# Contiguous operands in an edge sort, carried sums added once in DRAM, and a bias added by VectorE instead of TensorE

## The chip, the cores and the metric

The kernel runs on one core of one Trainium2 chip. Its time is the device time of one execution in microseconds (us), given as the median of several runs. The core has five engines with a queue of instructions each: TensorE (PE in the profile; PEld is its loading of weights), VectorE (DVE), ScalarE (ACT), GpSimd (POOL) and SyncE (SP). In this kernel SP issues the plain DMAs and POOL issues the indirect ones, which gather or scatter one row for each of 128 partitions.

## The reference

The reference is a graph block over 3125 nodes with 256 features. A normalised input goes through a message passing network over 103125 edges that are sorted by their target, and through a transformer of four layers with linear attention. Both are added to the input. On the sum, an attention over 65536 unsorted edges chooses two of four experts for each node, and each expert is a two-layer network.

```python
xn = _layernorm(x)
# message network: edges sorted by receiver (dst)
messages = concat(xn[src], edge_attr) @ W_message
agg = segment_sum(messages, dst, 3125)
h = layer_norm(relu(agg) + xn); three linear layers with skips; layer_norm
# transformer: 4 layers of linear attention (softmax of k over all nodes) + gelu feed-forward 256 -> 1024 -> 256
x = x + gnn + mix
# graph attention over 65536 unsorted edges gives scores for 4 experts
e = leaky_relu(a_src[src] + a_dst[dst]); alpha = segment softmax of e over dst
scores = layernorm(segment_sum(h[src] * alpha)); top 2 of 4, softmax
for ei in range(4):
    hh = gelu(xf @ W1[ei] + b1[ei])                 # 256 -> 512
    out = out + g[..., None] * (hh @ W2[ei] + b2[ei])   # 512 -> 256
x = x + out
```

## The kernel before

**Tiles.** The 3125 nodes are 25 tiles of 128 (the last holds 53), and they are worked on in seven chunks of up to four tiles (`CHUNKS`). The message edges lie on 128 partitions with 806 columns each; a partition holds a contiguous run of sorted edges. The attention's edges lie on 128 partitions with 512 columns each, which are worked on in 64 groups of eight columns (`GC`).

**The main line.** TensorE follows the transformer's four layers, chunk by chunk, with `ff_up` (L1101, then a gelu on ACT at L1102) and `ff_down` (L1112, added up at L1115). All other work is let in between by a planner: `pace()` adds up the planned time of what has been issued and lets in message columns (`run_columns`), pieces of message nodes and sends, and `beside()` takes jobs from a list. The order within each engine's queue follows from this, with some reordering when the program is compiled.

**The message sums.** POOL gathers a row of `xn` for each of the 806 columns (L478), and DVE adds each to a running sum that starts anew at a new target (L490). The running sums are written to `run_d` in DRAM. A node's sum is the running sum at its last edge. Since a target's edges can begin in one partition and end in the next, the last running sums of all partitions (`last_m`) are carried over. The nodes are then worked on in pairs of tiles (`pair`, a generator that is advanced piece by piece at each `yield`): `fetch` gathers the sums from `run_d` at the rows `sum_i` (L559), a mask `goes_on` (L569) times `last_m` gives the carried part (L571), L572 masks the fetched row by `has_m` and adds that part, and L575 adds `part`, which is read from `res_d`. Row block 0 of `res_d` is zero; the other blocks are filled only if the edges came unsorted, and `flag` picks which is read. After this follow transposes (L585), the message product (L593), three linear layers (L609 to L612), a normalisation, and the next `fetch`, three pairs ahead.

**The edge sort.** The attention's edges are brought in the order of their targets by counting. The target's number is split in `hi` (128 values) and `lo` (32 values). `count_group` makes one-hots of both by `one_hot` (L668, laid out as value by column, so that one column is read at a step of eight elements), multiplies them column by column (L683), has ACT copy the counts (L685), writes them to `counts_d` and adds them to `table` (L690). `place_group` reads the counts back (`parts`), turns them into running counts by a scan on DVE (L728), and adds up in one PSUM tile `look` for each edge how many come earlier: L746 with a constant, and at L753 eight products each with `near`, `run` and `earlier`. DVE picks each edge's own value at L755 and L756, and `laid` turns it into a place (`place`). ACT makes `earlier` from products at L740 by a Sign (L741). `send` (L770) scatters each column of edges to its place in `by_dst`, 512 times.

**The end of the mix.** `finish` adds the message network's result to `xm` (L805), normalises, and makes the attention's table (`tab`, L818 and L819).

**The experts.** `expert(e)` takes the chunks in turn: L1301 and a gelu (L1303), then for two tiles at a time L1309, which puts the second bias into PSUM as a product of ones with three bf16 parts of the bias (`bias_rows`, L145 to L151), and L1312. ACT takes the result out of PSUM (L1315 and L1317). Between them stand 16 edge chunks (`gathered`, L1211; `edge_chunk`, L1232 to L1269, with two exponentials on ACT at L1223). A tile with a `tag` shares the buffer of that tag with an earlier tile and must wait for its readers:

```python
be2s = [bias_rows(so, a["L0_ffn_b2"][e], f"be2{e}", tags) for e, tags in enumerate((
    ("own_bin", "lo", "base"), ("own_bin", "hi", "base"), ("own_bin", "place", "base"), ("own_bin", "ohT0", "base")))]
```

The functions that the diff touches, with the profile's line numbers:

Of the kernel before, what the change touches and what calls it, by code (L numbers as in the profile page):

```python
# [8 lines left out]
F32 = mybir.dt.float32  # L9
BF16 = mybir.dt.bfloat16  # L10
I32 = mybir.dt.int32
# [7 lines left out]
P = 128  # L19
# [39 lines left out]
def kernel(ctx: ExitStack, tc: tile.TileContext, a: dict, out: bass.AP):  # L59
# [124 lines left out]
    mi = mi_open.enter_context(tc.tile_pool(name="mi", bufs=1))  # L184
    res_d = dram.tile([P + NP, DM], F32, name="res_d")
    run_d = dram.tile([EP, DM], F32, name="run_d")
# [140 lines left out]
    nc.sync.dma_start(res_d[:P, :].rearrange("p (a b) -> p a b", b=160), zero[:, :160].rearrange("p (o c) -> p o c", o=1).to_broadcast([P, 2, 160]))  # L327
    pairs0 = so.tile([P, TE], I32, name="pairs0", tag="pairs")
# [25 lines left out]
    G.iota(bin_p, pattern=[[0, 1]], base=0, channel_multiplier=1, allow_small_or_imprecise_dtypes=True)  # L354
    ident_h = const.tile([P, P], F16, name="ident_h")
# [23 lines left out]
    has_m = state.tile([P, NT], F32, name="has_m")  # L379
# [7 lines left out]
    sums_ps = px.tile([P, LO * GC + 2 * NT], F32, name="sums_ps")  # L387

    table, whole_ps, first_ps = sums_ps[:, :LO * GC], sums_ps[:, LO * GC:LO * GC + NT], sums_ps[:, LO * GC + NT:]
# [33 lines left out]
    def ends_sum():  # L423
# [11 lines left out]
        cnt_d = dram.tile([1 + NP, 1], F32, name="cnt_d")  # L435
# [4 lines left out]
    def ends_done():  # L440
        V.tensor_tensor(has_m, cnt, own_n, op=ALU.is_gt)
        V.tensor_scalar(has_m, has_m, in_order, None, op0=ALU.mult)
        V.tensor_scalar(cnt, cnt, -1.0, 0.0, op0=ALU.add, op1=ALU.max)
        V.tensor_scalar(sum_i, cnt, float(EP - 1), None, op0=ALU.min)
# [56 lines left out]
    last_gather = [None]  # L501
# [38 lines left out]
    def message_nodes():  # L540
# [23 lines left out]
        def pair(c):  # L564
            agg = fetched[c[0]]
            k, n0, w = len(c), c[0] * P, len(c) * P
            for i, t in enumerate(c):
                goes_on = wk2.tile([P, P], F32, name="goes_on")
                V.tensor_scalar(goes_on, ids, last_t[:, t:t + 1], cont, op0=ALU.is_equal, op1=ALU.mult)  # L569
                ps = pg.tile([P, DM], F32, name="ps_g")  # L570
                T.matmul(ps, goes_on, last_m, start=True, stop=True)  # L571
                V.scalar_tensor_tensor(agg[:, i, :], agg[:, i, :], has_m[:, t:t + 1], ps, op0=ALU.mult, op1=ALU.add)  # L572
                part = wk2.tile([P, DM], F32, name="part", bufs=2)
                nc.sync.dma_start(part, res_d[bass.ds(flag * (P * (t + 1)), P), :])
                V.tensor_tensor(agg[:, i, :], agg[:, i, :], part, op=ALU.add)  # L575
                yield False
# [62 lines left out]

        for c in PAIRS[:3]:  # L640
            fetch(c)
# [29 lines left out]

    counts_d = dram.tile([GROUPS, P, LO * (GC + 1)], F16, name="counts_d")
# [5 lines left out]
    def count_group(t):  # L678
        if t < TE:
            ohh, ohl = one_hot(t, hi, P, "oh_hi", 2), one_hot(t, lo, LO, "oh_lo", 3)  # L680
            ps = pg.tile([P, LO, GC], F32, name="ps_g")
            for i in range(GC):
                T.matmul(ps[:, :, i], ohh[:, :, i], ohl[:, :, i], start=i == 0, stop=i == GC - 1, skip_group_check=True)  # L683
            cnt = cnts[t // GC % 2]
            S.copy(cnt[:, :, 1:], ps)  # L685
            nc.sync.dma_start(counts_d[t // GC, :, :], cnt.rearrange("p l i -> p (l i)"))
            counted.append((t, cnt))
        if t:
            t, cnt = counted.pop(0)
            T.matmul(table, ident_h, cnt[:, :, 1:], start=t == 0, stop=t + GC == TE, skip_group_check=True)  # L690
# [6 lines left out]
    def parts(t):  # L697
        cnt = so.tile([P, LO, GC + 1], F16, name="run", bufs=3)
# [3 lines left out]
    def starts():  # L702
        cnt2 = so.tile([P, LO], F32, name="cnt2", tag="base")
        V.tensor_reduce(cnt2, table.rearrange("p (l i) -> p l i", i=GC), AX.X, ALU.add)
# [13 lines left out]
    def place_group(t):  # L718

        late = looks.pop() if looks else None  # L720
        if t < TE:
# [4 lines left out]
            ohl = one_hot(t, lo, LO, "oh_lo", 3)  # L726
            near, run = places.pop()
            V.tensor_tensor_scan(run.rearrange("p l i -> p (l i)"), goes.rearrange("p l i -> p (l i)"),  # L728
                                 run.rearrange("p l i -> p (l i)"), 0.0, op0=ALU.mult, op1=ALU.add)
            if t + GC < TE:  # L730
                base = so.tile([P, LO], F32, name="base")
                V.tensor_tensor(base, run[:, :, GC], near, op=ALU.add)
# [10 lines left out]
        if late:  # L743
            t, ohT, ohl, near, run, earlier = late
            look = pg.tile([P, GC, LO], F32, name="ps_g")
            T.matmul(look.rearrange("p i l -> p l i"), all_h, ohl, start=True, stop=False, skip_group_check=True)  # L746
            for k in range(3):
                for i in range(GC):
                    if k == 2:
                        a1, a2 = earlier[:, i, :], ohl[:, :, i]  # L750
                    else:
                        a1, a2 = ohT[:P - 1, i, :], run[:P - 1, :, i] if k else near[:P - 1]
                    T.matmul(look[:, i, :], a1, a2, start=False, stop=k == 2, skip_group_check=True)  # L753
            own = so.tile([P, GC, LO], F32, name="own_bin", bufs=1)
            V.scalar_tensor_tensor(own, look, float(E2), ohl.rearrange("p l i -> p i l"), op0=ALU.add, op1=ALU.mult)  # L755
# [140 lines left out]
    def zero_fills():  # L896
        nothing = so.tile([P, TE], I32, name="nothing", tag="hr", bufs=2)
# [198 lines left out]
    def ff_up(l, c, h2, f0, f1):  # L1096
        w = len(c) * P
# [192 lines left out]
    def expert(e):  # L1290
# [4 lines left out]
        for c in CHUNKS:  # L1295
# [9 lines left out]
            for i0 in range(0, len(c), 2):  # L1305
# [3 lines left out]
                T.matmul(ps[:, :k, :], ones_b, be2[:, :k, :], start=True, stop=False, skip_group_check=True)  # L1309
                for i in range(k):  # L1310
                    for f in range(FF2 // P):
                        T.matmul(ps[:, i, :], hh[f][:, (i0 + i) * P:(i0 + i + 1) * P], we2[:, f, :],  # L1312
                                 start=False, stop=f == FF2 // P - 1, skip_group_check=True)
# [247 lines left out]
```

## Time and profile before

| what | value |
|---|---|
| median of 3 runs | 3781.26 us (3776.46 to 3784.04) |
| own time of the profiled execution | 3726.91 us |
| its span | 3725.2 us |
| mean granted TensorE clock | 0.762 |
| message gathers, L478 | 806 of 989 ns |
| sends, L770 | 512 of 966 ns |
| edge gathers, L1211 | 400 of 952 ns |

The profiled execution is some 54 us (1.4%) faster than the median of the runs shown. Its stages, in microseconds from the start of the span: start and normalisation 0 to 192, layer 0 to 930, layer 1 to 1472, layer 2 to 2333 (with an overlap of stages at its start), layer 3 and `finish` to 2892, experts and edge chunks to 3610, gates and output to 3725. The message gathers run from 42 to 1637, the count groups from 198 to 434, the place groups from 641 to 2766, the message nodes' pairs from 1687 to 2672 and the sends from 1638 to 2810.

A line of the profile gives the place of the instruction in the kernel (L12), its engine and operation, the tiles written and read, and the shapes. In a group's line follow the number of instructions, then busy time in us and the mean in ns of one, then the idle time of the engine just before them and what ended it. "issue" is time in which an engine waited for nothing that the profile shows, and "remote" is a release that the profile ascribes to no instruction. In a line of the timeline the first number is the start in us from the start of the span, the second the duration of the row, and the bracket at the end the idle time before it.

### The profile page before, as it was taken

How to read it: one execution, taken by the hardware profiler on the slowest of the kernel's cores; microseconds unless marked ns; L12 is line 12 of the kernel's file. 1: busy time of each engine (PE TensorE's matmuls, PEld its weight loads, DVE VectorE, ACT ScalarE, POOL GpSimd, SP SyncE). 2: the span in 40 equal slices, each digit the busy share in tenths (PEclk: the TensorE clock that was granted, in tenths of full speed). 3: DMA queues.
4: the chain of work that ended last, by engine and by line, in shares of the span. 5: the costliest groups of instructions: out<-in, count | busy, mean ns of one | idle time of the engine just before them, and what ended most of it. 6: DMA issues, size and time to landing. Idle time of an engine off the chain costs nothing. (4 is left out here: it accounts for less than half of the span.)

```text
span 3725.2 us, 31745 instructions
## 1 busy us (share of the span) xinstructions
PE 2232.7 (60%) x9891; PEld 1505.7 (40%) x9891; DVE 1452.2 (39%) x4484; ACT 1062.2 (29%) x1933; POOL 1776.0 (48%) x1843
## 2 busy tenths in 40 slices
PE   3667654675667676645575466547667275747470
PEld 2545433443444455433343344435445143424250
DVE  6656544644544455532232233324422021111127
ACT  4422242233233233322232224213333021212122
POOL 2545454544445544644435434453442736464623
PEclk8878776776778887877787777768788677868685
DMA  6656564746645556722010002101100101010101
GB/s 206 193 188 201 162 199 136 211 157 192 212 150 190 176 166 209 225 80 77 20 33 18 23 18 58 43 25 35 44 10 8 16 17 30 15 29 14 27 12 36
DMA packets 300669, 359.57 MB, mean 97 GB/s; under 512 B 180576, under 2 KB 248039, under 8 KB 287687
## 3 DMA queue, kind: packets, MB, share of 16 engines
q1 hardware_dynamic: 229782, 242.00, 20.4%
q0 software_dynamic: 70704, 115.42, 11.9%
q8 instruction: 80, 1.31, 0.1%
q14 instruction: 103, 0.84, 0.1%
HBM read 201.91 MB, written 155.35 MB: 96 GB/s over the span
## 5 line engine op out<-in xcount | busy, mean ns | idle before, releaser
L478 POOL DMA_INDIRECT m_run<-xn_d,src_i x806 | 797.5, 989 | 835.9 <-issue 228.2
L770 POOL DMA_INDIRECT by_dst<-pairs,place x512 | 494.8, 966 | 280.3 <-issue 185.5
L1211 POOL DMA_INDIRECT rows_c<-tab_d,si x400 | 380.6, 952 | 301.5 <-DVE rows_c L1269 182.6
L1101 PE MATMUL ps_a<-h,w 128*128 128x512 f32 (+1 forms) x896 | 413.0, 604 | 101.5 <-ACT gT L1102 38.5
L490 DVE SCALAR_TENSOR_TENSOR m_run<-m_run,stay 128x320 f32<-128x320 f32 x805 | 437.3, 543 | 32.3 <-DMA m_run<-xn_d,src_i 17.7
L1112 PE MATMUL ps_a<-w,gT 128*128 128x256 f32 x1600 | 382.3, 394 | 20.4 <-issue 19.9
L1112 PEld LDWEIGHTS ps_a<-w,gT 128*128 128x128 f32 x1600 | 314.4, 198 | 124.2 <-issue 78.4
L1301 PE MATMUL ps_a<-hT,we 128*128 128x512 f32 (+1 forms) x448 | 226.5, 640 | 137.9 <-issue 115.1
L1101 PEld LDWEIGHTS ps_a<-h,w 128*128 128x128 f32 x896 | 173.8, 214 | 267.5 <-issue 189.5
L1312 PE MATMUL ps_t<-we,hf 128*128 128x256 f32 x800 | 203.7, 406 | 111.6 <-issue 79.1
L609 PE MATMUL ps_a<-gh,gw 128*128 128x256 f32 (+1 forms) x312 | 106.4, 489 | 207.7 <-DVE gh L612 95.8
L1312 PEld LDWEIGHTS ps_t<-we,hf 128*128 128x128 f32 x800 | 160.2, 204 | 158.5 <-issue 97.9
L1301 PEld LDWEIGHTS ps_a<-hT,we 128*128 128x128 f32 x448 | 89.7, 213 | 294.0 <-issue 259.2
L1102 ACT ACTIVATE gT<-ps_a,b 128x512 f32<-128x512 f32 (+1 forms) x224 | 141.3, 641 | 214.3 <-PE ps_a L1101 118.8
L1261 DVE COPY rows_c<-ev 128x104 f32<-128x104 f32 (+1 forms) x16 | 4.6, 286 | 481.7 <-ACT ev L1223 471.3
L559 POOL DMA_INDIRECT aggr<-run_d,sum_i x25 | 24.4, 977 | 336.2 <-PE ps_t L585 312.9
L609 PEld LDWEIGHTS ps_a<-gh,gw 128*128 128x128 f32 x312 | 72.7, 250 | 235.9 <-DVE gh L612 102.2
L741 ACT ACTIVATE earlier<-ps_t,slope 128x512 f16<-128x512 f32 x128 | 93.8, 773 | 260.0 <-PE ps_t L740 146.2
L1039 PE MATMUL ps_g<-xm,kr 128*128 128x256 f32 x400 | 127.5, 463 | 63.8 <-ACT kr L1037 36.1
L123 ACT ACTIVATE hn<-xm,rstd 128x256 f32<-128x256 f32 x225 | 121.4, 592 | 86.5 <-DVE rstd L119 57.7
L1039 PEld LDWEIGHTS ps_g<-xm,kr 128*128 128x128 f32 x400 | 88.4, 232 | 118.3 <-ACT kr L1037 58.5
L159 PE MATMUL ps_t<-ident,hn 128*128 128x128 f32 x450 | 82.7, 319 | 87.6 <-issue 37.7
(399 smaller groups left out, 3615.6 us busy)
## 6 DMA issues: line engine op xcount, KB each, us to landing
run_d<-m_run SPq DMA_DIRECT2D x100, 1280.0 KB
m_run<-in_edge_attr_dram SPq DMA_DIRECT2D x95, 256.0 KB
hr<-row_h SPq DMA_DIRECT2D x64, 256.0 KB
m_run<-xn_d,src_i POOLq DMA_INDIRECT x806
w<-in_L_mix_W_dram SPq DMA_DIRECT2D x8, 1024.0 KB
by_dst<-pairs,place POOLq DMA_INDIRECT x512
rows_c<-tab_d,si POOLq DMA_INDIRECT x400
run_d<-rows_c SPq DMA_DIRECT2D x15, 312.0 KB
```

The lines of the kernel that those rows point to most:

```text
L123: S.activation(dst, src, AF.Identity, bias=r[:, 1, i:i + 1], scale=r[:, 0, i:i + 1])
L478: last_gather[0] = G.indirect_dma_start(out=m[:, t, :D], out_offset=None, in_=xn_d, in_offset=bass.IndirectOffsetOnAxis(ap=src_i[:, t0 + t ...
L490: add = V.scalar_tensor_tensor(m[:, t, :], before_m, stay[:, c:c + 1], m[:, t, :], op0=ALU.mult, op1=ALU.add)
L609: T.matmul(ps[:, :w], gw[i][:, kc, m * P:(m + 1) * P], h[:, kc, :w], start=kc == 0, stop=kc == 1)
L770: i = G.indirect_dma_start(out=by_dst, out_offset=bass.IndirectOffsetOnAxis(ap=place[:, t:t + 1], axis=0), in_=pairs0[:, t:t + 1], in_offs ...
L1039: T.matmul(ps_x[:, m, :], kr[:, m * P:(m + 1) * P], xm[:, t, :], start=i == 0 and m == 0, stop=i == len(c) - 1, skip_group_check=True)
L1101: T.matmul(ps[:, :w], ff_w[l]["w1"][:, kc, f * P:(f + 1) * P], h2[:, kc, :w], start=kc == 0, stop=kc == 1)
L1102: S.activation(gT[:, f, :w], ps[:, :w], AF.Gelu, bias=ff_w[l]["b1"][:, f:f + 1])
L1112: T.matmul(ps[:, i, :], gT[:, f, (2 * i0 + i) * P:(2 * i0 + i + 1) * P], ff_w[l]["w2"][:, f, :], start=False, stop=f == FF // P - 1, skip_ ...
L1211: G.indirect_dma_start(out=rows_c[:, t - COLS[j], :], out_offset=None, in_=tab_d, in_offset=bass.IndirectOffsetOnAxis(ap=si[:, t:t + 1], a ...
L1301: T.matmul(ps[:, :w], we1[:, kc, f * P:(f + 1) * P], hT[:, kc, c[0] * P:c[0] * P + w], start=kc == 0, stop=kc == 1)
L1312: T.matmul(ps[:, i, :], hh[f][:, (i0 + i) * P:(i0 + i + 1) * P], we2[:, f, :], start=False, stop=f == FF2 // P - 1, skip_group_check=True)
```

## The change

It has four parts.

1. In the sort, `low_hots` lays the one-hots of `lo` out as column by value, so that one column is contiguous; the counts' PSUM tile and the products L683, L746 and L753 follow. ACT's copy of the counts writes at a step of nine elements in place of DVE's and PE's strided reads, `table` has nine columns a value instead of eight, and in `place_group` ACT copies the scanned `run_l` to a contiguous `run_c`.
2. The carried sums are added once in DRAM: `carries` multiplies `last_m` by a mask `joined`, and one indirect DMA adds the result to the rows `carry_i` of `run_d`, before the first fetch. `ends_done` works out `carry_i`, and gives nodes without edges the zero row `NO_SUM`. The blocks that were read as `part` are copied behind `run_d` by 25 DMAs from DRAM to DRAM (in `zero_fills`). `pair` loses its first loop with a `yield` for each tile. With unsorted edges `sum_i` points to the copied rows.
3. The experts' second bias is a tile of 128 equal rows, loaded by SP; DVE adds it as it takes results out of PSUM. The bias products and `be2s` by `bias_rows` go.
4. `ff_up` leaves out the columns beyond node 3125 in the last chunk.

```diff
-    run_d = dram.tile([EP, DM], F32, name="run_d")
+    run_d = dram.tile([EP + NP + 1 + P, DM], F32, name="run_d")
...
     def ends_done():
-        V.tensor_tensor(has_m, cnt, own_n, op=ALU.is_gt)
-        V.tensor_scalar(has_m, has_m, in_order, None, op0=ALU.mult)
-        V.tensor_scalar(cnt, cnt, -1.0, 0.0, op0=ALU.add, op1=ALU.max)
-        V.tensor_scalar(sum_i, cnt, float(EP - 1), None, op0=ALU.min)
+        V.tensor_tensor(own_n, cnt, own_n, op=ALU.is_gt)
+        V.tensor_scalar(cnt, cnt, float(-1 - NO_SUM), None, op0=ALU.add)
...
+        V.tensor_tensor(sum_i, cnt, node_n, op=ALU.add)
+        at_i = small.tile([P, 1], I32, name="at_i", bufs=1)
+        V.tensor_scalar(at_i, lastd, 1.0, float(NP), op0=ALU.add, op1=ALU.min)
+        at = small.tile([P, 3], F32, name="at_end_of", bufs=1)
+        last_gather[0] = G.indirect_dma_start(out=at[:, 0:1], out_offset=None, in_=ends_at["d"],
+                                              in_offset=bass.IndirectOffsetOnAxis(ap=at_i, axis=0))
...
+        T.transpose(ps[:, :P], joined, ident)
...
+        T.matmul(ps[:, :1], sooner, ones[:, :1], start=True, stop=True)
...
+    def carries(pool):
+        ps = pg.tile([P, DM], F32, name="ps_g")
+        T.matmul(ps, joined, last_m, start=True, stop=True)
+        over = pool.tile([P, DM], F32, name="over")
+        V.tensor_copy(over, ps)
+        last_gather[0] = G.indirect_dma_start(out=run_d, out_offset=bass.IndirectOffsetOnAxis(ap=carry_i[:, :1], axis=0),
+                                              in_=over, in_offset=None, compute_op=ALU.add)
...
         def pair(c):
             agg = fetched[c[0]]
             k, n0, w = len(c), c[0] * P, len(c) * P
-            for i, t in enumerate(c):
-                goes_on = wk2.tile([P, P], F32, name="goes_on")
-                V.tensor_scalar(goes_on, ids, last_t[:, t:t + 1], cont, op0=ALU.is_equal, op1=ALU.mult)
-                ps = pg.tile([P, DM], F32, name="ps_g")
-                T.matmul(ps, goes_on, last_m, start=True, stop=True)
-                V.scalar_tensor_tensor(agg[:, i, :], agg[:, i, :], has_m[:, t:t + 1], ps, op0=ALU.mult, op1=ALU.add)
-                part = wk2.tile([P, DM], F32, name="part", bufs=2)
-                nc.sync.dma_start(part, res_d[bass.ds(flag * (P * (t + 1)), P), :])
-                V.tensor_tensor(agg[:, i, :], agg[:, i, :], part, op=ALU.add)
-                yield False
...
+        carries(wk2)
         for c in PAIRS[:3]:
             fetch(c)
...
+    def low_hots(t):
+        o = so.tile([P, GC, LO], F16, name="oh_lo", bufs=3)
+        V.tensor_tensor(o, low_ids.rearrange("p (o l) -> p o l", o=1).to_broadcast([P, GC, LO]),
+                        lo[:, t:t + GC].rearrange("p (t o) -> p t o", o=1).to_broadcast([P, GC, LO]), op=ALU.is_equal)
+        return o
...
     def count_group(t):
         if t < TE:
-            ohh, ohl = one_hot(t, hi, P, "oh_hi", 2), one_hot(t, lo, LO, "oh_lo", 3)
-            ps = pg.tile([P, LO, GC], F32, name="ps_g")
+            ohh, ohl = one_hot(t, hi, P, "oh_hi", 2), low_hots(t)
+            ps = pg.tile([P, GC, LO], F32, name="ps_g")
             for i in range(GC):
-                T.matmul(ps[:, :, i], ohh[:, :, i], ohl[:, :, i], start=i == 0, stop=i == GC - 1, skip_group_check=True)
+                T.matmul(ps[:, i, :], ohh[:, :, i], ohl[:, i, :], start=i == 0, stop=i == GC - 1, skip_group_check=True)
             cnt = cnts[t // GC % 2]
-            S.copy(cnt[:, :, 1:], ps)
+            S.copy(cnt[:, :, 1:].rearrange("p l i -> p i l"), ps)
...
-            T.matmul(table, ident_h, cnt[:, :, 1:], start=t == 0, stop=t + GC == TE, skip_group_check=True)
+            T.matmul(table, ident_h, cnt.rearrange("p l i -> p (l i)"), start=t == 0, stop=t + GC == TE, skip_group_check=True)
...
+            run = so.tile([P, GC, LO], F16, name="run_c", tag=f"counts{t // GC % 2}")
+            S.copy(run, run_l[:, :, :GC].rearrange("p l i -> p i l"))
...
-            T.matmul(look.rearrange("p i l -> p l i"), all_h, ohl, start=True, stop=False, skip_group_check=True)
+            T.matmul(look, all_h, ohl, start=True, stop=False, skip_group_check=True)
...
-                        a1, a2 = earlier[:, i, :], ohl[:, :, i]
+                        a1, a2 = earlier[:, i, :], ohl[:, i, :]
                     else:
-                        a1, a2 = ohT[:P - 1, i, :], run[:P - 1, :, i] if k else near[:P - 1]
+                        a1, a2 = ohT[:P - 1, i, :], run[:P - 1, i, :] if k else near[:P - 1]
...
     def zero_fills():
+        nc.sync.dma_start(run_d[DUMP:DUMP + P, :].rearrange("p (a b) -> p a b", b=160),
+                          zero[:, :160].rearrange("p (o c) -> p o c", o=1).to_broadcast([P, 2, 160]))
+        for t in range(NT):
+            nc.sync.dma_start(run_d[FALLEN + t * P:FALLEN + (t + 1) * P, :], res_d[bass.ds(flag * (P * (t + 1)), P), :])
...
     def ff_up(l, c, h2, f0, f1):
-        w = len(c) * P
+        w = min((c[-1] + 1) * P, N) - c[0] * P
...
-                T.matmul(ps[:, :k, :], ones_b, be2[:, :k, :], start=True, stop=False, skip_group_check=True)
...
-                    S.copy(y_all[:, e, ts[0]:ts[-1] + 1, :], ps[:, :k, :])
+                    y = y_all[:, e, ts[0]:ts[-1] + 1, :]
...
+                if len(y.shape) == 3 and y.shape[2] == P:
+                    V.tensor_tensor(y, ps[:, 0, :].rearrange("p (a d) -> p a d", a=2), be2.rearrange("p (a d) -> p a d", a=2), op=ALU.add)
+                else:
+                    V.tensor_tensor(y, ps[:, :k, :], be2.rearrange("p (o d) -> p o d", o=1).to_broadcast([P, k, D]), op=ALU.add)
...
-    be2s = [bias_rows(so, a["L0_ffn_b2"][e], f"be2{e}", tags) for e, tags in enumerate((
-        ("own_bin", "lo", "base"), ("own_bin", "hi", "base"), ("own_bin", "place", "base"), ("own_bin", "ohT0", "base")))]
+    be2s = []
+    for e, tag in enumerate(("lo", "hi", "own_bin", "ohT0")):
+        be2 = so.tile([P, D], F32, name=f"be2{e}", tag=tag)
+        nc.sync.dma_start(be2, a["L0_ffn_b2"][e].rearrange("(o n) -> o n", o=1).to_broadcast([P, D]))
+        be2s.append(be2)
```

## The prediction

> **What bounds the kernel now.** I read the page first, then busy time by stretches, the waits, the timeline around one pair of node tiles, and the groups for each edited line.
>
> ```profile
> span 3725.2 us, 31745 instructions
> PE 2232.7 (60%) x9891; PEld 1505.7 (40%) x9891; DVE 1452.2 (39%) x4484; ACT 1062.2 (29%) x1933; POOL 1776.0 (48%) x1843
> ```
>
> No engine is full. By stretches (length; busy of PE, PEld, DVE, ACT, POOL; granted clock; DMA share; GB/s), the transformer's layers 1, 2 and 3, then the experts:
>
> ```profile
> 930.00:1472.00 542.00, 365.34 (x1687) 253.60 (x1687) 274.38 (x713) 170.00 (x289) 268.73 (x274) 0.81 0.58 183
> 1683.00:2333.00 650.00, 380.49 (x1534) 258.67 (x1532) 182.85 (x538) 193.95 (x369) 287.62 (x299) 0.74 0.13 34
> 2333.00:2892.00 559.00, 357.59 (x1963) 255.51 (x1964) 182.56 (x635) 174.17 (x296) 232.10 (x240) 0.79 0.11 27
> 2892.00:3610.00 718.00, 423.20 (x1281) 251.93 (x1279) 126.82 (x680) 142.62 (x223) 382.07 (x402) 0.75 0.12 20
> ```
>
> PE is fullest nearly everywhere at some 60%; DVE and ACT have room; POOL's share is its indirect DMAs. Why PE isn't full shows in one pair's cycle:
>
> ```profile
> 1966.76 0.59 PE L609 MATMUL ps_a<-gh,gw 128*128 128x256 f32 x1 [0.62 <-issue]
> 1999.06 0.96 POOL L770 DMA_INDIRECT by_dst<-pairs,place  x1 [0.30 <-issue]
> 2006.02 1.45 ACT L164 ACTIVATE h<-ps_t,b1n,g 128x512 f32<-128x512 f32 x2 [41.82 <-remote]
> 2009.23 3.78 PE L609 MATMUL ps_a<-gh,gw 128*128 128x256 f32 x8 [33.60 <-DVE gh L612]
> 2026.48 0.99 POOL L559 DMA_INDIRECT aggr<-run_d,sum_i  x1 [26.46 <-PE ps_t L585]
> ```
>
> POOL issues 32 sends (0.96 + 0.30 us each, to 2000.0). While it does, PE, ACT and DVE nearly stop; some 6 us after the last send all run again, POOL now waiting 26.46 us for PE to release a buffer; then the next burst. Work progresses mainly in the quiet stretches, so what is shortened there counts, on PE first.
>
> **The change, part by part.** Durations are of this profiled execution: span 3725.2, own time 3726.9. The median of the three runs is 3781.3, 1.5% higher; the sum is made against 3726.9 and carried over by that ratio.
>
> *Products of the edge numbering (64 groups).* Contiguous and strided moving operands stand side by side:
>
> ```profile
> 2765.05 0.40 PE L753 MATMUL ps_g<-near,ohT 127*128 127x32 f16 x8
> 2765.30 0.71 PE L753 MATMUL ps_g<-run,ohT 127*128 127x32 f16 x8
> 2765.83 0.66 PE L753 MATMUL ps_g<-oh_lo,earlier 128*128 128x32 f16 x8
> ```
>
> Eight products take 0.40 us with `near` (contiguous), 0.71 with `run` (18-byte step), 0.66 with `oh_lo` (16-byte step). Both become contiguous: (0.31 + 0.26) x 64 = 36 us. L746, now contiguous at both ends, goes from 451 ns to perhaps L690's 318: 8 us. In the counts the moving operand becomes contiguous but the weights `oh_hi` keep their step and their loads (L683, 160 ns) are beside it: 0 to 18 us, taken 0.
>
> *Carried sums.* Gone from each of 25 node tiles:
>
> ```profile
> L571 PE MATMUL ps_g<-last_m,goes_on 128*128 128x320 f32 x50 | 21.8, 523 | 6.4 <-issue 3.2 <-DVE goes_on L569 3.1
> L572 DVE SCALAR_TENSOR_TENSOR aggr<-aggr,has_m,ps_g 128x320 f32<-128x320 f32 x25 | 13.6, 543 | 18.1 <-PE ps_g L571 11.9 <-issue 3.2 <-DMA aggr<-run_d,sum_i 2.6
> L575 DVE TENSOR_TENSOR aggr<-aggr,part 128x320 f32<-128x320 f32 x25 | 12.0, 482 | 0.0
> L569 DVE TENSOR_SCALAR goes_on<-ids,last_t,cont 128x128 f32<-128x128 f32 x25 | 8.6, 344 | 5.5 <-DMA run_d<-m_run 3.5 <-PE ps_g L571 1.9
> ```
>
> PE 21.8 us, DVE 34.2 us, and the hops between them: PE's waits for `goes_on` (8.3) and for the sum (16.1, in only two waits) come to 24 us, of which I take 20, since the transposes still wait for the fetch. DVE's 34 us lie mostly beside bursts: taken 5.
>
> *Experts' bias.* L1309's 48 products cost 21.5 us busy, but the next starts 0.21 us on: 10 us. The last chunk's up products narrow from 128 to 53 columns: L1101's own 329 ns against L981's 287, a product of 53 columns, give 42 ns x 128 = 5 us. PE's sum: 36 + 8 + 22 + 10 + 5 = 81 us. PE is busy 60% of the span, and I count that share: **-48 us**. Hops **-20**, DVE **-5**.
>
> The old bias tiles also go, and with them this stall:
>
> ```profile
> 2813.02 0.27 DVE L145 MEMSET be_parts<- 65x256 uint32 x1 [29.38 <-DMA by_dst<-pairs,place]
> 2815.79 1.89 PE L818 MATMUL ps_g<-wg,hT 128*128 128x16 f32 x8 [23.59 <-DVE tab L819]
> 2824.21 0.30 ACT L117 ACTIVATE rstd<-mv,eps 128x4 f32<-128x4 f32 x1 [32.29 <-DVE bst L109]
> ```
>
> One of them takes the buffer of `place`; its memset waits for the last sends to land, and behind it in DVE's queue stands `finish`, for which PE idles 23.6 us and ACT 32.3. The new tiles are written by SP alone, into buffers none of which is `place`'s. SP may wait for these, with the experts' weights queued behind it; but their last reader (L756, on `own_bin`) ends at 2768, before the stall begins at 2783.6. **-24 us**.
>
> *Added, DVE's one-hots and `own`.* Now L668 makes 1024 elements in 686 ns and 256 in 281: 0.53 ns an element and 146 fixed. `low_hots` repeats `lo` along the innermost axis. The Trainium skill ("VectorE: DVE Perf Modes", What auto-detection actually checks) gives a 16-bit operation two elements a cycle only if every tensor's step is one; a repeated operand has step zero. By the rule the copy takes 146 + 256 x 1.05 (the f32 rows' rate, L572) = 415 ns, 0.134 x 128 = +17 us; by the row's rate, nothing. That speaks against the change and I take the rule: +17 on DVE. `own` (L755, 596 ns) reads contiguously and could fall to L594's 420: -11. Half of the 6 in the open: **+3**.
>
> *Added, ACT.* Each place group gets `run_c`, 64 copies that read at 18-byte steps. Nearest rows: L685, same size, 372 ns; at worst L1315's 586 with twice the elements: 24 to 38 us. The count copy now writes at that step: 0 to 14 us. The same skill ("SBUF — State Buffer", Door 1) says that an access crossing to a new 16-byte line pays a penalty: by it the upper ends, 52 us, by the rows 24. ACT is 29% busy and I count a third of 36 between: **+12**. The hop matters too: `run_c` stands in ACT's in-order queue behind the scan, which waits for the counts' load (49.8 us in 7 waits), and gelus stand behind it. Most of that load is covered by a group's lead; with the cover gone, those 49.8 us reach ACT.
>
> *Added, once.* `ends_done` gets some ten small DVE operations, a transpose, a product and one POOL gather; `carries` a product, a copy and one scattering add on POOL. No row shows an adding scatter; the nearest is a plain send: 1.26 us with issue, up to 29 with the landing behind that memset, for which all fetches would wait: **+5**, near the lower end since the add comes well before the first sends. Besides, 27 small fills go to SP's queue, 25 of them 160-KB copies inside DRAM, ahead of `by_dst`'s fill, `run_d`'s writes and the loads of counts. They replace 25 loads of 160 KB. Moved from DMA share 0.11-0.13 to about 0.58, 8 MB of reading and writing at 183 GB/s is 44 us if nothing overlaps, 0 if the gaps take it: **+5**, towards the lower end, as POOL's gathers run well ahead of their sums (17.7 us of waiting in 805).
>
> *Experts, moved.* ACT loses 48 copies of 586 ns (28 us), DVE gets about as many adds like L1115's 687 (+33 us). POOL's chunks wait for DVE here; I take **+5**.
>
> Sum: -48 - 20 - 5 - 24 + 3 + 12 + 5 + 5 + 5 = -67, and of the shorter bursts' 50 us (first rival) a sixth, -8, since most of it should return later: **-75**. 3726.9 - 75 = 3652, times 1.0146 = 3705. With the DVE row in place of the rule, half of the 17 us goes: 3696.
>
> **The rivals.**
>
> *Shorter bursts, larger gain (0.20).* A pair advances by 15 yields, the change drops two; sends paced between fetches fall from 32 to about 28-29, 3.5 x 1.26 = 4 us in each of 13 cycles, -50 us; with PE's 81 counted whole (-33 more) the time is near 3620. For: the burst is when PE halts. Against: the 50 sends put off must go out later in layer 3.
>
> *Hidden (0.16).* What is removed lay inside bursts, and only the stall goes, half repaid: near 3760 (3735 to 3785). For: PE idles 40% anyway. Against: 23.6 and 32.3 us of idling were measured behind the memset.
>
> *DVE couples the experts; slower (0.14).* Now:
>
> ```profile
> DVE rows_c L1261 <- ACT ev L1223: 471.3, 15, 50.3
> POOL rows_c L1211 <- DVE rows_c L1269: 182.6, 10, 33.2
> ```
>
> (sum, count, longest.) DVE stands at L1261 until ACT's exp, and exp stands among gelus. With the adds on DVE, PE's results wait in that same queue, exp waits for the 3.7 us of DVE work (L1232 to L1254) after an add, and PE's three `ps_a` buffers hold six products of L1301, some 5 us. 3.7 us for each of 16 edge chunks is +59; if the whole chain of 9 us is exposed it is +144, and the time near 3781 - 80 + 146 = 3847. It decides from 80 / 16 = 5 us per chunk. For: 471 us of waiting at that line. Against: three buffers, and DVE busy 18% there.
>
> **How the numbers follow.** The forecast has 0.50, at 3705, itself 3660 to 3750. A difference under about 0.2%, 7.6 us, can't be told from none. Faster: 0.49 + 0.20 + 0.08 = 0.77; same: 0.01 + 0.06 = 0.07; slower: 0.02 + 0.14 = 0.16. The range 3595 to 3805 leaves out the lower fringe of the bursts' rival and most of the slower one.
>
> **What would show it.** L753's `run` and `oh_lo` products at 0.40 us a group; no product with `last_m` in the pairs; no memset waiting near the end of layer 3, and PE's 23.6 us gone; low one-hots near 415 ns; `run_c` at 370-590 ns; fewer sends between fetches. Wrong if the experts' stretch is longer than 718 us (the slower rival), if layer 1 grows beyond 542 by tens of us (the copies), or if layers 2 and 3 (1209 us) shrink by less than 30 (hidden) or over 130 (bursts).

## The result, and the profile after

The changed kernel takes 3724.2 us (median of four runs, 3715.5 to 3738.3) where the kernel before takes 3778.9. The ratio is 0.9861, with a 95% interval of 0.9825 to 0.9897, so 1.4% faster: 53 us by the ratio, 55 between the medians. In a second series, with six runs of it beside eleven of before, it was 0.9883 (0.9847 to 0.9919). The prediction had -75 us and 3705 with a range of 3595 to 3805. The sign and the range held, but several of its terms did not, as the experiments show. A few timed executions that took over 1.5% longer than the fastest of the same kernel count as slow and are left out of the ratios.

One caution stands ahead of every reading below. The profiled executions of the kernel before took 3726.9 us here and 3744.5 when it was profiled again, while its timed runs lie around 3770 (fifty of them between 3731.9 and 3791.4 in one series). The profiled executions of the changed kernel took 3723.1 and 3714.1, much nearer to its timed median. So the profiles show only a part of the gain; sizes are taken from the timed ratios, and the profiles say where it can be seen.

The page after, first two lines:

```profile
span 3721.3 us, 31510 instructions
PE 2185.9 (59%) x9794; PEld 1482.9 (40%) x9794; DVE 1452.1 (39%) x4425; ACT 1137.5 (31%) x1955; POOL 1783.6 (48%) x1845
```

PE has 47 us less to do, ACT 75 us more, DVE the same (the page before stands in the prediction). That ACT's load grew by more than PE's fell, and the kernel still got faster, is the first thing to see.

Three stretches, cut by POOL's work: from the first to the last message gather, from there to the last send, and from the end of `finish` to the end (columns as in the prediction). Before:

```profile
43.00:1638.00 1595.00, 1035.32 (x4998) 712.71 (x4996) 837.58 (x2214) 500.98 (x939) 796.83 (x806) 0.78 0.59 184
1638.00:2812.00 1174.00, 680.23 (x3200) 468.93 (x3200) 345.35 (x1070) 343.99 (x621) 527.02 (x546) 0.75 0.12 32
2889.00:3724.00 835.00, 442.00 (x1348) 266.25 (x1346) 208.01 (x900) 165.76 (x272) 433.81 (x461) 0.72 0.12 22
```

After:

```profile
42.00:1649.00 1607.00, 1035.08 (x5005) 712.85 (x5003) 846.37 (x2215) 579.79 (x978) 799.18 (x807) 0.77 0.59 185
1649.00:2792.00 1143.00, 660.89 (x3146) 449.33 (x3146) 309.52 (x977) 368.29 (x655) 532.02 (x547) 0.75 0.11 30
2870.00:3720.00 850.00, 413.99 (x1296) 262.51 (x1294) 239.72 (x953) 137.22 (x220) 436.22 (x463) 0.71 0.12 21
```

The middle stretch, with the message nodes' pairs, the sends and the place groups of layers 2 and 3, lost 31 us. The gathers' stretch did not shrink in the profile, and the last one, where PE works 28 us less, did not either.

What POOL waits for in the middle stretch (sum in us, number of waits, longest), before and after:

```profile
POOL aggr L559 <- PE ps_t L585: 312.9, 10, 43.3
POOL by_dst L770 <- issue: 184.0, 503, 30.9
POOL by_dst L770 <- DVE rstd L118: 38.1, 1, 38.1
POOL by_dst L770 <- DVE place L660: 36.8, 2, 30.5
POOL by_dst L770 <- DVE base L732: 19.9, 1, 19.9
```

```profile
POOL aggr L595 <- PE ps_t L611: 178.1, 8, 30.4
POOL by_dst L805 <- issue: 154.2, 506, 0.3
POOL by_dst L805 <- DVE place L687: 112.9, 4, 56.0
POOL by_dst L805 <- DVE base L767: 46.0, 1, 46.0
POOL aggr L595 <- PE ps_t L775: 40.5, 1, 40.5
POOL run_d L480 <- DVE over L479: 20.3, 1, 20.3
POOL by_dst L805 <- DVE run L728: 13.8, 1, 13.8
POOL aggr L595 <- DMA run_d<-over,carry_i: 6.1, 1, 6.1
```

The pairs release their buffers earlier: the fetches' waits for PE fall from 313 us to 219 (178 at the pairs' transposes and, new, 41 at a transpose of the place groups). But the sends now wait for the place groups: at `place`, `base` and `run` together 173 us, where it was 57, or 95 with the 38 put down to `rstd`. The last fetch starts some 130 us earlier than before, and the last send ends only 20 us earlier (37 between the second profiles of the two kernels). So most of what the pairs gave up has become a new wait. What the stretch lost has the size of one wait of 30.9 us at a send, for which the profile names no releaser ("issue") and which is gone after.

The three rows of the place products, and the edited groups:

```profile
2671.36 0.36 PE L788 MATMUL ps_g<-near,ohT 127*128 127x32 f16 x8
2671.57 0.35 PE L788 MATMUL ps_g<-run_c,ohT 127*128 127x32 f16 x8
2671.77 0.35 PE L788 MATMUL ps_g<-oh_lo,earlier 128*128 128x32 f16 x8
```

```profile
L718 ACT CAST counts<-ps_g 128x256 f16<-128x256 f32 x64 | 79.8, 1404 | 66.4 <-remote 27.1 <-PE ps_g L716 22.6 <-issue 9.1
L701 DVE TENSOR_TENSOR oh_lo<-low_ids,lo 128x256 f16<-128x256 f16 x128 | 52.8, 415 | 0.0
L764 ACT COPY run_c<-run 128x256 f16<-128x256 f16 x64 | 41.8, 656 | 96.5 <-remote 62.5 <-PE ps_g L788 17.6 <-PE ps_a L1052 7.8
L790 DVE SCALAR_TENSOR_TENSOR own_bin<-ps_g,oh_lo 128x256 f32<-128x256 f32 x64 | 26.8, 420 | 214.3 <-remote 172.6 <-PE ps_g L788 26.7 <-PE ps_a L1052 12.0
```

All three sets of eight products now take 0.35 or 0.36 us, where `run` took 0.71 and `oh_lo` 0.66. The one-hot takes 415 ns, which is the size that the prediction worked out for it, and `own` 420. The surprise is the first row: ACT's copy of the counts, written at an 18-byte step, takes 1404 ns where it took 372.

### The profile page after: what moved, and what is told of

It is laid out like the page before. It is cut to its first block, busy times and chain, and to the rows that moved or that the text cites. A ratio compares the mean times of both kernels' runs of the same rounds, so it can differ in the third digit from the quotient of the medians.

```text
span 3721.3 us, 31510 instructions
## 1 busy us (share of the span) xinstructions
PE 2185.9 (59%) x9794; PEld 1482.9 (40%) x9794; DVE 1452.1 (39%) x4425; ACT 1137.5 (31%) x1955; POOL 1783.6 (48%) x1845
## 5 line engine op out<-in xcount | busy, mean ns | idle before, releaser
L1151 PE MATMUL ps_a<-w,gT 128*128 128x256 f32 x1600 | 392.6, 399 | 24.2 <-issue 23.5
L1340 PE MATMUL ps_a<-hT,we 128*128 128x512 f32 (+1 forms) x448 | 205.4, 605 | 226.1 <-ACT hf L1342 128.3
L1078 PE MATMUL ps_g<-xm,kr 128*128 128x256 f32 x400 | 136.8, 488 | 117.9 <-issue 61.7
L1342 ACT ACTIVATE hf<-ps_a,be 128x512 f32<-128x512 f32 (+1 forms) x112 | 69.7, 641 | 384.4 <-remote 239.5
L1361 DVE TENSOR_TENSOR y_all<-ps_t,be 128x512 f32<-128x512 f32 (+1 forms) x39 | 26.0, 668 | 334.0 <-PE ps_t L1350 119.2
L1052 PE MATMUL ps_a<-wq,h 128*128 128x256 f32 x400 | 119.0, 434 | 61.6 <-issue 25.6
```

The source lines that it names most:

```text
L1052: T.matmul(ps[:, i, :], h1[:, kc, o + i * P:o + (i + 1) * P], att_w[l]["wq"][:, kc, :], start=kc == 0, stop=kc == 1)
L1078: T.matmul(ps_x[:, m, :], kr[:, m * P:(m + 1) * P], xm[:, t, :], start=i == 0 and m == 0, stop=i == len(c) - 1, skip_group_check=True)
L1151: T.matmul(ps[:, i, :], gT[:, f, (2 * i0 + i) * P:(2 * i0 + i + 1) * P], ff_w[l]["w2"][:, f, :], start=False, stop=f == FF // P - 1, skip_ ...
L1340: T.matmul(ps[:, :w], we1[:, kc, f * P:(f + 1) * P], hT[:, kc, c[0] * P:c[0] * P + w], start=kc == 0, stop=kc == 1)
```

## The experiments

The theory carried in from the prediction is that each part contributes its own terms: work on PE counts by PE's share, the hops count, ACT and DVE have room. The rivals were that the planner's shorter bursts make the gain, that DVE couples the experts, and that the gain returns at the sends' end. Each ratio below is to the kernel before, in the same series.

### The kernel before, again

Edit: none.

> The kernel before, run once more as if it were a change. Its profiled execution took 3726.9 us while its timed runs took 3771 to 3784; the change's took 3723.1 in a profile and 3715 to 3738 when timed. If the profile of before was one quick execution, a second one should come out near 3775 and show where the 50 us lie; if profiled executions of this kernel are always quicker, again near 3727. The ratio should be 1.000 within its interval, whose width says what five rounds can tell.

Measured: 1.0012 (0.9987 to 1.0038), and 3744.5 us in its profiled execution. So some 20 runs beside some 50 can tell a quarter of a per cent, or 10 us. The two profiled executions of this kernel are quicker than the timed medians beside them, by 54 and 28 us. Two are too few for a rule, and a few timed runs are as quick (the lowest took 3727.3 us); the cause is not known.

### The sort alone

Edit: the parts of the diff in `low_hots`, `count_group`, `parts`, `starts` and `place_group`, and no other. In `parts` the buffers for the counts read back (`run`) also go from three to two, which the diff shown ahead leaves out.

> Only the contiguous operands of the sort. The prediction's terms: PE -44 us at 60% is -27, DVE +3, ACT +12: -12 us, near 3767. If PE's shortening is hidden behind the sends' bursts and ACT's copy is not: 0 to +15. If contiguous operands are the heart of the change: -50.

Measured: 0.9915 (0.9892 to 0.9938), that is -32 us (-41 to -23), almost three times the forecast and neither of the other two cases. Its stretches, in its own profile:

```profile
42.00:1628.00 1586.00, 1018.20 (x5000) 701.42 (x4998) 846.66 (x2216) 579.62 (x977) 800.63 (x807) 0.77 0.59 185
1628.00:2811.00 1183.00, 676.36 (x3200) 460.67 (x3200) 342.88 (x1070) 360.13 (x649) 527.14 (x545) 0.74 0.12 32
```

In the gathers' stretch, which holds all count groups and 34 of the 64 place groups, PE is busy 17 us less than in the profile of before and the stretch is 9 us shorter (18 against the second profile of before). The sends' stretch, at 1183 us, lies between the 1174 and 1186 of the two profiles of before.

### The carries alone

Edit: the parts of the diff in `run_d`, `ends_done`, `carries`, `pair` and `zero_fills`, and no other.

> Only the carried sums added once in DRAM. The prediction's terms: PE 22 us at 60% is -13, hops -20, DVE -5, added once +10, shorter bursts -8: -36 us, near 3743. If the shorter bursts count in full: -80. If what is taken out of the pairs comes back where the sends are finished in layer 3: within 10 us of before, with the last feed-forward of layer 3 earlier by 50 us or more and the last send not.

Measured: 0.9862 (0.9806 to 0.9918), -52 us (-73 to -31). Its gathers' and its sends' stretch:

```profile
43.00:1659.00 1616.00, 1041.25 (x5004) 715.93 (x5003) 837.68 (x2215) 501.33 (x939) 803.80 (x807) 0.78 0.58 184
1659.00:2810.00 1151.00, 680.82 (x3152) 468.01 (x3152) 317.57 (x1003) 355.49 (x629) 531.16 (x546) 0.75 0.11 29
```

The sends' stretch is 1151 us where the two profiles of before have 1174 and 1186, and PE's busy time in it is the same (680.8 us against 680.2 and 677.6). So what the stretch lost is not time in which PE was busy. What the carries also took out are the mask, the product and the two DVE operations between fetch and transposes, which each pair had to go through before POOL got its buffer back, and 28 us of DVE's work in the stretch (345 to 318). Which of these it is was not tested one by one. The gathers' stretch grew: 1616 us against 1595 and 1604, of which more below.

### The bias alone

Edit: the part of the diff in `expert` and `be2s`, and no other.

> Only the experts' second bias: added by DVE, and no bias tile in the buffer of place. The prediction's terms: PE 10 us at 60% is -6, the stall at the end of layer 3 -24, the move to DVE +5: -25 us, near 3754. If DVE's queue couples the experts: the experts' stretch grows by 50 us or more and the kernel is slower by 20 or more.

Measured: 1.0012 (0.9983 to 1.0041), no change. The stall at the memset is gone, and this is what stands in its place (timeline at the end of layer 3 of this kernel):

```profile
2832.21 1.04 PE L818 MATMUL ps_g<-wg,hT 128*128 128x16 f32 x4 [18.94 <-issue]
2838.51 1.03 PE L818 MATMUL ps_g<-wg,hT 128*128 128x16 f32 x4 [4.22 <-ACT hT L162]
2839.15 0.17 DVE L819 COPY tab<-ps_g 128x16 f32<-128x16 f32 x1 [41.04 <-PE ps_g L818]
2848.00 0.30 ACT L117 ACTIVATE rstd<-mv,eps 128x4 f32<-128x4 f32 x1 [8.25 <-DVE bst L109]
```

DVE now waits 41 us for PE, and PE waits 19 us for nothing that the profile names, until the last send goes out (2832.5). From the last send to the last copy of `tab` it is some 77 us in the two profiles of before, 79 here and 78 in the changed kernel. So the memset did not set the time at which PE goes on: without it PE stands as long beside the last burst. What holds PE there the profile doesn't name. Nor does DVE couple the experts: the last stretch is 835 us here and 835 and 832 in the profiles of before, though PE's busy time in it falls by 28 us.

### The changed kernel, again

Edit: the whole diff.

> The changed kernel once more, beside the others of this call, for a ratio over more runs. The sort alone gave 0.9915 and the carries alone 0.9862, the bias alone 1.0012; if the parts add up the whole is at 0.979 (3690 us beside 3770), if they take out the same idle time it stays near 0.986 (3717).

Measured: 0.9883 (0.9847 to 0.9919), -44 us. The parts, -32, -52 and +5, sum to -79 with an uncertainty of some 25; the whole brings 44 to 53, near the second case (the parts take out the same idle time); the first lies at the edge of the uncertainties.

### The yields kept

```diff
             k, n0, w = len(c), c[0] * P, len(c) * P
+            for t in c:
+                yield False
```

> The changed kernel with an empty yield for each tile kept at the start of a pair, so that the planner advances the pairs in 15 steps as before and puts as many sends between two fetches as before (32). If the dropped work is what counts, the time stays within 10 us of the changed kernel. If the shorter bursts made a good part of the gain, it loses 20 us or more. If the sends put off to layer 3's end cost more than the shorter bursts bring, it gains 10 us or more.

Measured: 0.9884 (0.9850 to 0.9918), the same as the changed kernel in the same series. The sends between fetches are again 31, 39, 27, 38, 29, 35, 24, 27 and 33, exactly those of before (mean 31), where the changed kernel has 30, 27, 32, 25, 32, 25, 33, 14 and 23 (mean 27). So the bursts did become shorter as forecast: after the last fetch come 245 sends in the changed kernel, 196 before and here. The time is the same within some 19 us, which excludes the 50 of the bursts' rival, though not a few us.

### Sort and carries

Edit: the diff without the bias by DVE and without the narrower last chunk; run in two series.

> Sort and carries without the bias by DVE and the narrower last chunk. If the parts add up: 0.978, near 3687. If the bias by DVE costs time only in company of the others (its adds behind the edge chunks in DVE's queue, after an earlier end of the mix), this is faster than the changed kernel by 10 us or more; if the bias is free, the two are within 10 us.

> Sort and carries without the bias by DVE, once more, as the base for the next three, which are made from it. Before it gave 0.9841 (0.9809 to 0.9873); the same is expected, near 3713 beside 3773.

Measured: 0.9841 (0.9809 to 0.9873) and 0.9858 (0.9814 to 0.9902), -60 and -53 us. This is the changed kernel or a little better: in the one series that has both, 0.9841 stands against 0.9883, 16 us less with an uncertainty of some 18. So it is not settled whether the bias by DVE is free or costs some us in company. Neither run reached the 0.978 of parts that add up.

### The counts as before

```diff
-            ohh, ohl = one_hot(t, hi, P, "oh_hi", 2), low_hots(t)
-            ps = pg.tile([P, GC, LO], F32, name="ps_g")
+            ohh, ohl = one_hot(t, hi, P, "oh_hi", 2), one_hot(t, lo, LO, "oh_lo", 3)
+            ps = pg.tile([P, LO, GC], F32, name="ps_g")
...
-                T.matmul(ps[:, i, :], ohh[:, :, i], ohl[:, i, :], start=i == 0, stop=i == GC - 1, skip_group_check=True)
+                T.matmul(ps[:, :, i], ohh[:, :, i], ohl[:, :, i], start=i == 0, stop=i == GC - 1, skip_group_check=True)
...
-            S.copy(cnt[:, :, 1:].rearrange("p l i -> p i l"), ps)
+            S.copy(cnt[:, :, 1:], ps)
```

> The changed kernel, the count groups alone as before: DVE's one-hot at 281 ns, PE's product with a strided moving operand at 243 ns, ACT's copy contiguous at 373 ns in place of 1404. If ACT's 66 us more of copying in layer 0 delay the counts: faster by 15 us or more. If ACT's room hides them and PE's products count: slower by up to 10. If neither matters: within 5 us.

Measured: 0.9858 (0.9817 to 0.9899), against 0.9883 for the changed kernel: 9 us less, with an uncertainty of some 20. The three cases can't be told apart: ACT's 66 us more of copying in layer 0 cost anything from nothing to some 30 us.

### Idle products in the pairs

The base of this run and of the next two is the kernel with sort and carries; the edits are shown against it.

```diff
             k, n0, w = len(c), c[0] * P, len(c) * P
+            for t in c:
+                ps = pg.tile([P, DM], F32, name="ps_g")
+                for _ in range(8):
+                    T.matmul(ps, ident, last_m, start=True, stop=True)
```

> The base with eight idle products of 320 columns added at the start of each of the 25 node tiles (200 products, whose results nobody reads; some 272 ns apart, 54 us of PE). If POOL's bursts and PE's work take turns, so that the time is POOL's transfers and the gaps in which PE works: slower by 54 us or more, 1.4%. If PE's work counts at its 60% share: 33 us. If it is hidden beside POOL's bursts: under 10 us.

Measured: 1.0000 (0.9972 to 1.0028) against 0.9858 for its base: +54 us, with an uncertainty of some 20. The expectation's size has a fault, which the group's line shows:

```profile
L606 PE MATMUL ps_g<-last_m,ident 128*128 128x320 f32 x400 | 121.0, 445 | 0.4 <-DVE own_bin L794 0.4
1659.00:2856.00 1197.00, 754.53 (x3546) 520.27 (x3546) 316.24 (x1003) 367.06 (x653) 530.60 (x547) 0.79 0.11 28
```

A 32-bit product runs as two instructions, so it is 400 of them, 269 ns from start to start, 108 us of PE and not 54. The cases are then 108 us if POOL's bursts and PE's work simply take turns, 65 at a share of 60%, and under 10 if hidden. The measured 54 is a share of one half. The second line shows it in the profile as well: the sends' stretch is 1197 us, 53 more than its base's 1144, for 97 us more of busy PE. POOL's waits for the pairs' transposes, in the base and here, show where it went:

```profile
POOL aggr L595 <- PE ps_t L611: 183.4, 8, 30.7
POOL aggr L595 <- PE ps_t L615: 241.4, 9, 36.6
```

The added products stand just ahead of these transposes, and the waits grow by 58 us. So the half holds for work at this place, on the way to POOL's buffer. It was not measured for PE's work in the sort or the experts.

### More copies on ACT

```diff
             S.copy(run, run_l[:, :, :GC].rearrange("p l i -> p i l"))
+            for _ in range(2):
+                S.copy(run, run_l[:, :, :GC].rearrange("p l i -> p i l"))
```

> The base with the copy run_c made three times (128 more strided copies of 656 ns, 84 us of ACT). If ACT's room hides them: within 10 us of the base. If ACT's work counts by a third, as the prediction had it: slower by 28 us. If the hop from DVE's scan over ACT to PE is on the path: slower by 60 us or more.

Measured: 0.9890 (0.9853 to 0.9927), +12 us against the base, with an uncertainty of some 20, for 84 us more of ACT. By the middle value a seventh counts, but the interval reaches from nothing to more than a third. The 60 us of a hop on the path are excluded; the 28 us of a third are within the uncertainty.

### No strided copies at all

```diff
-            S.copy(cnt[:, :, 1:].rearrange("p l i -> p i l"), ps)
+            S.copy(cnt[:, 1:, :], ps)
...
-        cnt = so.tile([P, LO, GC + 1], F16, name="run", bufs=2)
+        cnt = so.tile([P, GC + 1, LO], F16, name="run", bufs=3)
...
-            V.tensor_tensor_scan(run_l.rearrange("p l i -> p (l i)"), goes.rearrange("p l i -> p (l i)"),
-                                 run_l.rearrange("p l i -> p (l i)"), 0.0, op0=ALU.mult, op1=ALU.add)
-            run = so.tile([P, GC, LO], F16, name="run_c", tag=f"counts{t // GC % 2}")
-            S.copy(run, run_l[:, :, :GC].rearrange("p l i -> p i l"))
+            for to, by in ((slice(1, 8, 2), slice(0, 7, 2)), (slice(3, 8, 4), slice(1, 6, 4)), (slice(7, 8), slice(3, 4)),
+                           (slice(5, 6), slice(3, 4)), (slice(2, 7, 2), slice(1, 6, 2))):
+                V.tensor_tensor(run[:, to, :], run[:, to, :], run[:, by, :], op=ALU.add)
```

> The base with the counts laid out column by value also in DRAM, so that ACT's count copy is contiguous (near 373 ns in place of 1404), and the running counts made by five short adds on DVE in place of the scan, so that no run_c is needed. ACT loses 66 + 42 us, DVE gets some 0.3 us more a group (20 us in all). If ACT's work is hidden and DVE's too: within 8 us of the base. If the ACT hop in the place groups delays PE: faster by 20 us or more. If DVE counts: slower by 10 to 20.

Measured: 0.9830 (0.9782 to 0.9879) against the base's 0.9858: 11 us less, with an uncertainty of some 25, which decides between none of the three cases. The edit also gives `run` its third buffer back. The copy is back at 373 ns and `run_c` is gone:

```profile
L718 ACT CAST counts<-ps_g 128x256 f16<-128x256 f32 x64 | 22.7, 373 | 92.1 <-remote 25.5 <-PE ps_g L716 25.3 <-DMA counts_d<-counts 19.2
```

It has the lowest ratio of all, but no version here is faster than the changed kernel beyond the intervals.

## Why the prediction was right, and where it was not

**The sum.** -75 was forecast, 44 to 53 measured, so the range held. That it held is in part luck, since errors in both directions met. Alone, the sort and the carries brought 84 us where -48 was forecast for them, and the bias nothing where -25 was. Together the parts brought less than one by one. By arithmetic the stall's -24 is the whole gap (the same sum without it is -51), but with the other terms as far off that agreement proves nothing.

**The stall.** The prediction said "its memset waits for the last sends to land, and behind it in DVE's queue stands `finish`." The line was read rightly, the conclusion was not. The wait was real and so were the idle times behind it, but with the memset taken away as much time appears as PE's "issue" and DVE's wait for PE. The prediction had described that very standstill for the pairs' cycle and did not ask whether it held here.

**PE's sum and share.** 81 us of PE's work were to go, at a share of 60%. The share measured with the idle products is one half (54 us of 108, uncertainty some 20), which agrees, but for the pairs alone; in the experts PE's 28 us less moved nothing. The sum was too large by the pages: PE is busy 2185.9 and 2174.5 us after where it was 2232.7 and 2241.4, which is 47 to 67 less. With the carries alone it is not less at all (2243.8), though 22 us of products are gone. Why the whole falls by less than the rows is not shown.

**The sort.** Its PE terms were of the right size by the rows (0.35 us for eight products, 308 ns for L781, together some 52 us where 44 were forecast), but PE's busy time as a whole fell only by 17 to 25 us in the sort alone (2216.1). DVE's one-hot came out at the 415 ns worked out for it. ACT was mis-sized in two ways that oppose each other. Its copies cost 42 + 57 us more, not 24 to 52: `run_c` takes 656 ns, and the count copy, for which 0 to 14 us was allowed, 1404 ns. And ACT's room seems to swallow most of it (12 us of 84 in the test; a third, as was taken, is not excluded). Together -32 alone, where -12 was forecast. Even without any cost on ACT the forecast would have been -24; where the rest comes from is not known.

**The carries.** -36 was forecast (PE -13, hops -20, DVE -5, added once +10, bursts -8) and -52 measured, with -36 inside its interval. The shares are off: shorter bursts bring nothing that can be measured, as the kept yields show, and PE's busy time in the sends' stretch did not fall. What is left are the hops and DVE's work between fetch and transposes. That a longer way to the transposes costs time, the idle products show; how much of the -52 comes from the hops is argued, not shown. "Added once" was mis-sized too. The added POOL gather in `ends_done` was costed at its issue; it waits for the write of `cnt_d`, and every message gather behind it on POOL waits too:

```profile
POOL at_end_of L460 <- DMA cnt_d<-cnt_n: 28.7, 1, 28.7
```

This wait is there in every profile with the carries, at 26 to 29 us. And the gathers' stretch is longer with the carries: 1616 us against 1595 and 1604 of before, and 1607 and 1609 in the changed kernel against 1586 in the sort alone. So some 12 to 23 us seem to go there, where +5 was allowed. The adding scatter costs 1.60 us, and the fetch behind it waits 6.1 us for it to land. Its 20.3 us before that is the wait for the last running sums, where the first fetch of before waited 19.0. The 25 copies inside DRAM left no trace that I could find. Putting the gather behind the last message gather was not tried.

**The rivals.** "Shorter bursts" at its 50 us is refuted by the kept yields, and "DVE couples the experts" at 20 us or more by the bias alone. That the gain returns at the sends' end is right in good part: the last fetch is some 130 us earlier, the last send 20 to 37. "Hidden" is right for the bias and the stall, wrong for the other two parts.

**The signs.** Those for the change itself came, except that `run_c` at 656 ns lies above the 370 to 590 given for it, and that of PE's 23.6 us some 19 came back under another name. Of the three signs of being wrong, the experts' stretch shows up in one profile: from the last copy of `tab` to the first gather of the gates it is 736 us after, where before has 723. In the second profiles it is 723 and 719, and 722 with the bias alone, so it doesn't carry the slower rival. Layers 2 and 3, from the copy to `last_m` to the last copy of `tab`, shrank by 32 us (1206 to 1174) and 41 (1217 to 1176), little more than the 30 below which "hidden" was to hold. Layer 1 is some 550 us in all four profiles.

**What stays open.** The parts sum to -79 and the whole brings 44 to 53; sort and carries together bring 53 to 60 where their sum is 84. These gaps are about as large as their uncertainties, so it may be that little or nothing is lost in company. The new waits for places can't be the reason, since the carries' own profile has them in full. The narrower last chunk was never run alone; its forecast of 3 us is below what these runs can tell. Where the sort's gain lies, and why both profiled executions of before are quicker than most of its timed ones, isn't settled.

## What to carry to other kernels

Before a wait is booked as a gain, ask what else stands still in that time: if the engines named behind it are held up by the same burst, taking the wait away only renames it. Cost a small indirect DMA by what it waits for and what is queued behind it, not by its issue. Where several engines fill each other's gaps, shortening a dependent chain can bring a gain where the busy time of the fullest engine does not fall (the carries), and an engine with room can take a layout change that looks dear in its own row (the count copy).

## What was not expected of the hardware

- ACT writing 256 16-bit results at an 18-byte step took 1404 ns against 373 contiguous, about 4 ns more an element. Reading 16-bit elements at that step and writing them contiguously took 656 ns.
- PE reading 16-bit operands at a step of 16 or 18 bytes took 0.66 to 0.71 us for eight products of 32 columns, against 0.35 to 0.40 contiguous.
- The timed runs of one kernel spread over 1.6% (3731.9 to 3791.4 us), and its two profiled executions (3726.9 and 3744.5 us) lay at or below the lower end of that.
- While POOL issues a run of sends, the other engines can come to a full stand: from 1980 to 2005 us of the profile before, PE, DVE and ACT have no busy time at all; the last send of that burst starts at 1999.1. The cause is not known.
